# A recurrent layer's first run, moved beside the projection of its inputs and accumulated in PSUM

## The chip, the cores and the metric

The kernel runs on one core of one Trainium2 chip. The metric is the device time of one execution in microseconds (us); lower is better. The engines are named as in the profile: PE (TensorE, the matrix unit; PEld is its weight load), DVE (VectorE), ACT (ScalarE), POOL (GpSimd) and SP (SyncE, which only starts transfers here).

## The reference

A layer of two parts works on x with B = 2 sequences, T = 2048 steps and D = 256 features. First comes a normalized recurrent network, then attention with 8 heads of width 64 whose values and outputs are mixed from 5 experts each. Only the recurrent part is touched by the change:

```python
def _L0_attn_ref(x, Wi, bi, Wh, bh):
    xi = jnp.einsum('btd,hd->bth', x, Wi) + bi
    def step(h, xt):
        h_new = jnp.tanh(xt + h @ Wh.T + bh)
        return (h_new, h_new)
    h0 = jnp.zeros((x.shape[0], Wh.shape[0]), dtype=x.dtype)
    _, hs = jax.lax.scan(step, h0, jnp.swapaxes(xi, 0, 1))
    return jnp.swapaxes(hs, 0, 1)
...
x = x + _L0_attn_ref(_layernorm(x, axis=-1), ...)
x = x + _L0_ffn_ref(_layernorm(x, axis=-1), ...)
```

The entries of Wh are drawn with a spread of 0.02, so a state's influence fades quickly with the steps that follow it.

## The kernel before

All data are fp32. The kernel does not walk through 2048 steps one after the other. It cuts each sequence into 128 segments (NS) of 16 consecutive steps (S), and does step s of all 128 segments at once: one "chunk" c holds the 16-step position c of all segments of both sequences, 128 x 2 columns. The recurrent part then has these stages, in this order:

1. *Projection of inputs* (lines 277 to 335). For each of the 16 chunks: DVE measures mean and variance (`measure`), POOL normalizes, PE transposes (four 128x128 transposes, line 300), ACT copies the transposed chunk out of PSUM (line 302), PE multiplies it with Wi (two halves mc of the features, two halves kc of the contraction, line 309, 256 columns each), and ACT writes the sum plus both biases to `xi` in SBUF (line 316). The loop issues the transposes of chunk c+1 ahead of the projection of chunk c. `ps_xi` has three PSUM buffers for the products and `ps_t` three for the transposes.
2. *Run a, from zero states* (`run("a", ...)`, line 534, and `step`, line 358). It starts all segments from zero at position `SKIP` = 3, where the state is just tanh of `xi` (line 362), and does the positions 4 to 15 with one step each. A step does, for each batch b and each feature half mc, two matmuls with Wh over 128 columns (line 368), an addition of `xi` on DVE (line 375) and a tanh on ACT (line 376). Only the last states are kept, in `ends`, one column further to the right, so that the end of a segment becomes the start of the next.
3. *Run b* (`run("b", ...)`, line 535). It begins with the states in `ends` and does all 16 positions in the same way, keeping every state in `hs`. Beside it (`beside`, line 470) the states are transposed back, added to x on POOL, stored to DRAM, and normalized for the attention.
4. `compare` (line 505) subtracts the last states of run a from those of run b. If any of the 65,536 differs by more than `TOL` = 4 x 2^-23, a flag is set, and the whole pass is done again with `slow` set, where the segments are run 128 times over.

The attention follows, from about 110 us to the end; it is one long software-pipelined loop whose order is written out by hand.

Every stage touched here is under a manual schedule: each engine takes its instructions in the order in which the program writes them, and waits at each for what it needs. A matmul that waits holds back everything behind it on PE.

Of the kernel before, what the change touches and what calls it, by code (L numbers as in the profile page):

```python
# [8 lines left out]
F32 = mybir.dt.float32  # L9
I32 = mybir.dt.int32  # L10
AF = mybir.ActivationFunctionType
# [3 lines left out]
P = 128  # L15
EPS = 1e-5
PSUM = bass.MemoryType.PSUM
# [3 lines left out]
def pass_over(  # L21
# [17 lines left out]
    nc = tc.nc  # L39
    tc_pool, mark = tc.tile_pool, "s" if slow else ""  # L40

    def tile_pool(name, **kw):
        return tc_pool(name=name + mark, **kw)

    B, T, D = x.shape
    E, _, DH = Wv.shape
    H = Wq.shape[1] // DH
    KC = D // P
    NCH = T // P
# [32 lines left out]
    wh = rconst.tile([P, KC, D], F32, name="wh")  # L82
    bias = rconst.tile([P, 2, KC], F32, name="bias")
    bsum = rconst.tile([P, KC], F32, name="bsum")
# [42 lines left out]
    def misc(shape, nm):  # L127
        return ps_m.tile(shape, F32, tag="m", name=nm)
# [54 lines left out]
    def stats(pool, mv, src, nm):  # L183

        st = pool.tile([P, 6], F32, tag="ln_st", name=f"st{nm}")
        nc.vector.bn_stats(st, src)
        nc.vector.bn_aggr(mv, st)
# [26 lines left out]
    def scales(pool, mv, n, nm):  # L214

        neg, v, y = guess(pool, mv, n, nm)
        return neg, newton(pool, v, y, n, range(3), nm)

    def normalize(dst, src, neg, y, k, eng=nc.gpsimd):
        eng.tensor_scalar(  # L220
            dst, src, neg[:, k : k + 1], y[:, k : k + 1], ALU.add, ALU.mult
        )
# [39 lines left out]

    S = NCH
    NS = P
    NEWTON = 3


    rst = rw.enter_context(tile_pool(name="rst", bufs=1))
    xi = rst.tile([P, KC, S, B, NS], F32, name="xi")
    hs = rst.tile([P, KC, S, B, NS], F32, name="hs")  # L270

    ends = rst.tile([P, KC, B, NS + 1], F32, name="ends")
    ones = rst.tile([P, 1], F32, name="ones")
# [2 lines left out]

    with tile_pool(name="prep", bufs=3) as pp, tile_pool(
        name="lna", bufs=3
    ) as lnp, tile_pool(name="ps_xi", bufs=3, space=PSUM) as ps_xi, tile_pool(
        name="ps_t", bufs=3, space=PSUM  # L280
    ) as ps_t, tc.manual_schedule():
        norm_of, turned = {}, {}

        def measure(c0, n):
            mv = pp.tile([P, n * B, 2], F32, tag=f"mv{n}", name=f"mva{c0}")
            for c in range(c0, c0 + n):
                for b in range(B):
                    stats(lnp, mv[:, (c - c0) * B + b, :], xt[c][:, b, :], f"a{c}_{b}")
            neg, y = scales(lnp, mv, n * B, f"a{c0}")
            for c in range(c0, c0 + n):  # L290
                norm_of[c] = neg, y, (c - c0) * B

        def turn_in(c):
            neg, y, k = norm_of.pop(c)
            xn = pp.tile([P, B, D], F32, tag="xn", bufs=2, name=f"xn{c}")
            tp = ps_t.tile([P, KC, B, P], F32, tag="tp", name=f"tpa{c}")
            for b in range(B):
                normalize(xn[:, b, :], xt[c][:, b, :], neg, y, k + b)
                for kc in range(KC):
                    nc.tensor.transpose(tp[:, kc, b, :], xn[:, b, kc * P : (kc + 1) * P], ident)  # L300
            turned[c] = pp.tile([P, KC, B, P], F32, tag="xnT", bufs=2, name=f"xnT{c}")
            nc.scalar.copy(turned[c], tp)

        def project_in(c):
            xnT = turned.pop(c)
            for mc in range(KC):
                px = ps_xi.tile([P, B, P], F32, tag="px", name=f"px{c}_{mc}")
                for kc in range(KC):
                    nc.tensor.matmul(  # L309
                        px.rearrange("p b n -> p (b n)"),  # L310
                        lhsT=wi[:, kc, mc * P : (mc + 1) * P],
                        rhs=xnT[:, kc].rearrange("p b n -> p (b n)"),
                        start=kc == 0,
                        stop=kc == KC - 1,
                    )
                nc.scalar.activation(xi[:, mc, c], px, AF.Identity, bias=bsum[:, mc : mc + 1])

        groups, c0 = [], 0
        for n in (1, 1, 2, 3, 4, 5):
            groups.append((c0, n))  # L320
            c0 += n
        assert c0 == NCH
        measure(*groups.pop(0))
        nc.vector.tensor_tensor(bsum, bias[:, 0, :], bias[:, 1, :], ALU.add)
        for c in range(NCH):
            while groups and groups[0][0] <= c + 2:
                measure(*groups.pop(0))
            if c == 0:
                turn_in(0)
            if c < 2:  # L330
                project_in(c)
            if c + 1 < NCH:
                turn_in(c + 1)
            if c >= 2:
                project_in(c)

# [8 lines left out]

    TOL = 4 * 2.0**-23
    GC = NCH // 2
    SKIP = 3  # L350
    sp = rw.enter_context(tile_pool(name="step", bufs=3))
    lnp = rw.enter_context(tile_pool(name="ln", bufs=2))
    ps_t = ctx.enter_context(ExitStack())
# [3 lines left out]

    def step(nm, s, prev, h, ps_h):
        for b in range(B):
            if prev is None:  # L360
                for mc in range(KC):
                    nc.scalar.activation(h[:, mc, b, :], xi[:, mc, s, b, :], AF.Tanh)
                continue
            pre = sp.tile([P, KC, NS], F32, tag=f"pre{b}", name=f"pre{nm}_{s}_{b}")
            for mc in range(KC):
                ph = ps_h.tile([P, NS], F32, tag=f"ph{b}_{mc}", name=f"ph{nm}_{s}_{b}_{mc}")
                for kc in range(KC):
                    nc.tensor.matmul(  # L368
                        ph,
                        lhsT=wh[:, kc, mc * P : (mc + 1) * P],  # L370
                        rhs=prev(kc, b),
                        start=kc == 0,
                        stop=kc == KC - 1,
                    )
                nc.vector.tensor_tensor(pre[:, mc, :], ph, xi[:, mc, s, b, :], ALU.add)
                nc.scalar.activation(h[:, mc, b, :], pre[:, mc, :], AF.Tanh)  # L376

    def run(nm, from_zero, keep_states, ps_h, beside=None):
        prev = None if from_zero else (lambda kc, b: ends[:, kc, b, 0:NS])
        for s in range(SKIP if from_zero else 0, S):  # L380
            if keep_states:
                h = hs[:, :, s]
            elif s == S - 1:
                h = ends[:, :, :, 1:]
            else:
                h = sp.tile([P, KC, B, NS], F32, tag="h", name=f"h{nm}_{s}")
            step(nm, s, prev, h, ps_h)
            if beside:
                beside(s)
            prev = lambda kc, b, h=h: h[:, kc, b, :]  # L390

    def turn_back(c, nm):

        tp = pst.tile([P, B, KC, P], F32, tag="tp", name=f"tpb{nm}{c}")
        for b in range(B):
            for kc in range(KC):
                nc.tensor.transpose(tp[:, b, kc, :], hs[:, kc, c, b, :], ident)
        hv_of[c] = sp.tile([P, B, D], F32, tag="hv", bufs=2, name=f"hv{nm}{c}")
        nc.scalar.copy(hv_of[c], tp.rearrange("p b c d -> p b (c d)"))

    def add_back(c, eng):

        eng.tensor_tensor(xt[c], xt[c], hv_of.pop(c), ALU.add)  # L403
        nc.sync.dma_start(out=x1d[c], in_=xt[c])
# [4 lines left out]
    def roots(mv, n, nm, pool=lnp, split=False):  # L409
# [14 lines left out]
        yield  # L424
        for k in range(NEWTON):
            if y is None:
# [92 lines left out]
    with tile_pool(name="ps_h", bufs=1, space=PSUM) as ps_h:  # L519
        if slow:  # L520
            nc.gpsimd.memset(hs[:, :, S - 1], 0.0)
            with tc.For_i(0, NS, 1):
                nc.vector.tensor_copy(ends[:, :, :, 1:], hs[:, :, S - 1])
                run("c", False, True, ps_h)
            for c in range(S):
                turn_back(c, "c")
                add_back(c, nc.gpsimd)
                stats_back(c, "c")
            *_, root_of[0] = roots(mv2[0], GC, "c")
            for c in range(0, GC, 2):  # L530
                xn_of[c] = norm_back(c, "c", pool2)
        else:
            with tc.manual_schedule():
                run("a", True, False, ps_h)
                run("b", False, True, ps_h, beside)
                turn_back(S - 1, "b")
                for c in (S - 2, S - 1):
                    add_back(c, nc.vector)
                    stats_back(c, "b")
# [478 lines left out]
    for u, (i, n) in enumerate(units):  # L1018
        b, h = heads[i]
# [241 lines left out]
```

## Time and profile before

| | |
|---|---|
| Median of three runs | 1560.38 us (1559.92 to 1560.54) |
| Profiled execution | 1562.38 us |
| Its span, first to last instruction | 1560.5 us |
| PE busy | 1513.2 us (97%) |
| DVE busy | 1300.0 us (83%) |
| POOL busy | 1287.0 us (82%) |
| ACT busy | 1245.4 us (80%) |
| Projection of inputs | 0 to about 52.2 us |
| Run a | 52.9 to 74.4 us |
| Run b and what is beside it | 74.5 to about 110 us |
| Attention | to 1560.5 us |

The page of the profile lists engines, waits and the costliest groups of instructions. A name such as `px<-xnT,wi` is the tile that is written and those that are read; L309 is line 309 of the kernel. Nearly all of the span is attention, so shares over the span say little about the stages before it; those are read from the view by stretches of time and from the timelines of single engines. An fp32 matmul of the program shows as two records.

### The profile page before, as it was taken

How to read it: one execution, taken by the hardware profiler on the slowest of the kernel's cores; microseconds unless marked ns; L12 is line 12 of the kernel's file. 1: busy time of each engine (PE TensorE's matmuls, PEld its weight loads, DVE VectorE, ACT ScalarE, POOL GpSimd, SP SyncE). 2: the span in 40 equal slices, each digit the busy share in tenths (PEclk: the TensorE clock that was granted, in tenths of full speed). 3: DMA queues.
4: the chain of work that ended last, by engine and by line, in shares of the span. 5: the costliest groups of instructions: out<-in, count | busy, mean ns of one | idle time of the engine just before them, and what ended most of it. 6: DMA issues, size and time to landing. Idle time of an engine off the chain costs nothing.

```text
span 1560.5 us, 41474 instructions
## 1 busy us (share of the span) xinstructions
PE 1513.2 (97%) x17582; PEld 534.4 (34%) x17582; DVE 1300.0 (83%) x1811; ACT 1245.4 (80%) x1617; POOL 1287.0 (82%) x855
## 2 busy tenths in 40 slices
PE   6999899999999999999999999999999999999988
PEld 5984222222233333333223332222222222222233
DVE  7474899999988877888987779999999999899873
ACT  4674688888888888888887778888888888888863
POOL 3154699999999987999997778899999999999970
PEclk9999999999999999999999999999999999999999
DMA  5021478888888887788786777888888888888963
GB/s 167 1 109 40 114 163 196 190 189 176 177 178 179 183 183 162 163 178 179 160 200 156 167 161 176 175 178 176 175 177 179 175 179 180 174 170 176 195 163 92
DMA packets 86821, 254.15 MB, mean 163 GB/s; under 512 B 11808, under 2 KB 31072, under 8 KB 86624
## 3 DMA queue, kind: packets, MB, share of 16 engines
q0 software_dynamic: 43488, 164.65, 57.9%
q1 hardware_dynamic: 41504, 86.13, 16.6%
q8 instruction: 140, 2.29, 0.6%
q10 hardware_dynamic: 1632, 0.61, 0.2%
q14 instruction: 57, 0.47, 0.1%
HBM read 59.46 MB, written 50.33 MB: 70 GB/s over the span
## 4 chain that ended last, share of the span: by engine, by line
PE 63%; DVE 19%; ACT 7%; issue 5%; DMA 3%; POOL 1%; ACTq 0%; SPq 0%; DVEq 0%; POOLq 0%
PE s L642 21%; PE o L723 17%; DVE m L664 11%; ACT p L654 5%; PE d L744 4%; DVE pro L789 3%; PE pq L166 3%; PE pk L147 3%; PE pz L885 2%; PE phb L368 2%; PE px L309 1%; PE pha L368 1%; DMA p<-p 1%; DMA z<-x1d 1%; ACT p L713 1%
## 5 line engine op out<-in xcount | busy, mean ns | idle before, releaser
L710 POOL TENSOR_TENSOR p<-p,top 128x1024 f32<-128x1024 f32 x378 | 1005.1, 2759 | 25.8 <-ACT top L703 25.5
L654 ACT COPY p<-s 128x1024 f32<-128x1024 f32 x512 | 511.5, 1012 | 139.6 <-issue 60.8
L713 ACT ACTIVATE p<-p 128x1024 f32<-128x1024 f32 x512 | 538.8, 1064 | 51.3 <-DVE p L710 42.7
L642 PE MATMUL s<-q,k 64*32 64x512 f32 x4096 | 501.6, 596 | 4.9 <-ACT p L654 2.5
L642 PE MATMUL s<-qs,k 64*32 64x512 f32 x4096 | 501.6, 596 | 3.5 <-ACT p L654 1.8
L723 PE MATMUL o<-p,v 128*32 128x512 f32 x4096 | 492.4, 598 | 5.1 <-DVE os L760 4.3
L664 DVE TENSOR_TENSOR m<-s,m 128x1024 f32<-128x1024 f32 x320 | 390.7, 1221 | 85.5 <-PE s L642 76.1
L735 POOL DMA_DIRECT2D p<-p x254 | 259.9, 1023 | 103.2 <-issue 43.7
L723 PEld LDWEIGHTS o<-p,v 128*32 128x32 f32 x4096 | 114.0, 109 | 301.5 <-issue 158.9
L642 PEld LDWEIGHTS s<-q,k 64*32 64x32 f32 x4096 | 100.5, 106 | 156.0 <-ACT p L654 60.3
L642 PEld LDWEIGHTS s<-qs,k 64*32 64x32 f32 x4096 | 100.4, 106 | 154.2 <-ACT p L654 58.1
L710 DVE TENSOR_TENSOR p<-p,pt 128x1024 f32<-128x1024 f32 x126 | 152.4, 1210 | 0.0
L744 PE MATMUL d<-p,ones 128*32 128x512 f32 x1032 | 136.3, 592 | 1.6 <-DMA p<-p 1.6
L664 DVE TENSOR_TENSOR m<-s,p 128x1024 f32<-128x1024 f32 x64 | 78.4, 1225 | 50.5 <-ACT p L654 49.6
L789 DVE TENSOR_TENSOR pro<-po,mr 128x1280 f32<-128x1280 f32 (+1 forms) x67 | 95.9, 1431 | 3.2 <-DVE mr L785 0.5
L626 DVE TENSOR_TENSOR xq<-xq,wp 128x1280 f32<-128x1280 f32 x60 | 89.2, 1487 | 2.1
L632 DVE TENSOR_REDUCE v<-xq 128x256 f32<-128x1280 f32 x60 | 88.5, 1475 | 0.0
L166 PE MATMUL pq<-xn2T,wq 128*32 128x512 f32 x512 | 62.2, 598 | 0.0
L147 PE MATMUL pk<-xn2T,wk 128*32 128x512 f32 x512 | 61.5, 598 | 0.0
L744 PEld LDWEIGHTS d<-p,ones 128*32 128x32 f32 x1032 | 34.0, 110 | 79.9 <-issue 76.0
L843 POOL DMA_DIRECT2D yd<-pro x48 | 60.1, 1252 | 0.0
L403 POOL TENSOR_TENSOR x<-x,hvb 128x512 f32<-128x512 f32 x14 | 17.8, 1275 | 45.8 <-ACT hs L376 34.2
(178 smaller groups left out, 1492.3 us busy)
## 6 DMA issues: line engine op xcount, KB each, us to landing
p<-p POOLq DMA_DIRECT2D x254, 512.0 KB, 5.4
xq<-xvd SPq DMA_DIRECT2D x60, 640.0 KB, 4.3
yd<-pro POOLq DMA_DIRECT2D x48, 640.0 KB, 6.5
qs<-q SPq DMA_DIRECT2D x64, 128.0 KB, 4.8
yd<-pro SPq DMA_DIRECT2D x8, 640.0 KB, 5.9
y<-yd SPq DMA_DIRECT2D x8, 640.0 KB, 8.2
x<-in_x SPq DMA_DIRECT2D x16, 256.0 KB, 5.8
x1d<-x SPq DMA_DIRECT2D x16, 256.0 KB, 2.0
```

The lines of the kernel that those rows point to most:

```text
L147: nc.tensor.matmul(pk[at_col : at_col + 32], lhsT=wk[:, kc, h * DH + g : h * DH + g + 32], rhs=xc[:, kc, c0 // 2 : (c0 + HC) // 2, o, :], ...
L166: nc.tensor.matmul(pq[at_col : at_col + 32, :], lhsT=wq[:, kc, h * DH + g : h * DH + g + 32], rhs=xn2T[:, kc, b, n * QB : (n + 1) * QB], s ...
L626: nc.vector.tensor_tensor(xq, xq, wp.unsqueeze(2).to_broadcast([P, 4, DH, E]), ALU.mult)
L642: nc.tensor.matmul(ss[g : g + 32, o, :], lhsT=k_of[i][half, c, g : g + 32], rhs=q_of[i, n][o][half, :], start=True, stop=True, tile_positi ...
L654: nc.scalar.copy(p, ss)
L664: nc.vector.tensor_tensor(m, ss, ring[t - 1] if c == 1 else m, ALU.max)
L710: eng.tensor_tensor(p, p, top.unsqueeze(1).to_broadcast([P, 2, QB]), ALU.subtract)
L713: nc.scalar.activation(ring[t], ring[t], AF.Exp)
L723: nc.tensor.matmul(o_of[u][at_col : at_col + 32, :], lhsT=v_of[i][:, 2 * c + o, g : g + 32], rhs=ring[t][:, o, :], start=c == 0, stop=c == ...
L735: nc.gpsimd.dma_start(out=ring[t], in_=ring.pop(t + 1), accum_op=ALU.add)
L744: nc.tensor.matmul(den_of[u][32 * g : 32 * (g + 1), :], lhsT=ones32, rhs=ring[(t, t1)[g // 2]][:, g % 2, :], start=first, stop=last, tile_ ...
L789: nc.vector.tensor_tensor(dst, po[:, s : s + n, 0:DH].unsqueeze(2).to_broadcast([P, n, E, DH]), mr[:, s : s + n].unsqueeze(3).to_broadcast ...
```

## The change

Run a no longer follows the projection. A new function `first_run` does one position of it inside the projection's loop, one chunk behind. It multiplies the previous state of all 256 columns (both batches) with Wh straight onto the PSUM tile that holds that chunk's projection, without the start flag, and ACT takes tanh of the sum, with the biases, from PSUM. ACT still writes `xi` from the same tile first, since run b needs it. So that a PSUM bank is not shared, each product tile takes a full bank; there are six of them, and the transposes use the two buffers of the shared pool `misc` instead of three of their own. `run` and `step` keep only what run b and the repeated pass need. The order on PE in the loop becomes: transposes of chunk c+1, projection of chunk c, recurrent matmuls of chunk c-1.

```diff
@@ -262,6 +262,7 @@
     S = NCH
     NS = P
+    SKIP = 3
     NEWTON = 3
@@ -276,10 +277,8 @@
     with tile_pool(name="prep", bufs=3) as pp, tile_pool(
         name="lna", bufs=3
-    ) as lnp, tile_pool(name="ps_xi", bufs=3, space=PSUM) as ps_xi, tile_pool(
-        name="ps_t", bufs=3, space=PSUM
-    ) as ps_t, tc.manual_schedule():
-        norm_of, turned = {}, {}
+    ) as lnp, tile_pool(name="ps_xi", bufs=6, space=PSUM) as ps_xi, tc.manual_schedule():
+        norm_of, turned, px_of, h_of = {}, {}, {}, {}
@@ -293,7 +292,7 @@
-            tp = ps_t.tile([P, KC, B, P], F32, tag="tp", name=f"tpa{c}")
+            tp = misc([P, KC, B, P], f"tpa{c}")
@@ -303,17 +302,42 @@
         def project_in(c):
             xnT = turned.pop(c)
+            px_of[c] = []
             for mc in range(KC):
-                px = ps_xi.tile([P, B, P], F32, tag="px", name=f"px{c}_{mc}")
+
+                px = ps_xi.tile([P, 512], F32, tag="px", name=f"px{c}_{mc}")[:, : B * P]
                 for kc in range(KC):
                     nc.tensor.matmul(
-                        px.rearrange("p b n -> p (b n)"),
+                        px,
                         lhsT=wi[:, kc, mc * P : (mc + 1) * P],
                         rhs=xnT[:, kc].rearrange("p b n -> p (b n)"),
                         start=kc == 0,
                         stop=kc == KC - 1,
                     )
+                px = px.rearrange("p (b n) -> p b n", b=B)
                 nc.scalar.activation(xi[:, mc, c], px, AF.Identity, bias=bsum[:, mc : mc + 1])
+                px_of[c].append(px)
+
+        def first_run(c):
+
+            pxs, prev = px_of.pop(c), h_of.pop(c - 1, None)
+            if slow or c < SKIP:
+                return
+            h = ends[:, :, :, 1:]
+            if c < S - 1:
+                h = pp.tile([P, KC, B, NS], F32, tag="h", bufs=2, name=f"ha_{c}")
+            for mc, px in enumerate(pxs):
+                for kc in range(KC if prev is not None else 0):
+                    nc.tensor.matmul(
+                        px,
+                        lhsT=wh[:, kc, mc * P : (mc + 1) * P],
+                        rhs=prev[:, kc],
+                        start=False,
+                        stop=kc == KC - 1,
+                        skip_group_check=True,
+                    )
+                nc.scalar.activation(h[:, mc], px, AF.Tanh, bias=bsum[:, mc : mc + 1])
+            h_of[c] = h
@@ -333,6 +357,9 @@
             if c >= 2:
                 project_in(c)
+            if c:
+                first_run(c - 1)
+        first_run(NCH - 1)
@@ -357,10 +383,6 @@
     def step(nm, s, prev, h, ps_h):
         for b in range(B):
-            if prev is None:
-                for mc in range(KC):
-                    nc.scalar.activation(h[:, mc, b, :], xi[:, mc, s, b, :], AF.Tanh)
-                continue
@@ -375,15 +397,10 @@
-    def run(nm, from_zero, keep_states, ps_h, beside=None):
-        prev = None if from_zero else (lambda kc, b: ends[:, kc, b, 0:NS])
-        for s in range(SKIP if from_zero else 0, S):
-            if keep_states:
-                h = hs[:, :, s]
-            elif s == S - 1:
-                h = ends[:, :, :, 1:]
-            else:
-                h = sp.tile([P, KC, B, NS], F32, tag="h", name=f"h{nm}_{s}")
+    def run(nm, ps_h, beside=None):
+        prev = lambda kc, b: ends[:, kc, b, 0:NS]
+        for s in range(S):
+            h = hs[:, :, s]
             step(nm, s, prev, h, ps_h)
@@ -521,7 +538,7 @@
-                run("c", False, True, ps_h)
+                run("c", ps_h)
@@ -531,8 +548,7 @@
             with tc.manual_schedule():
-                run("a", True, False, ps_h)
-                run("b", False, True, ps_h, beside)
+                run("b", ps_h, beside)
```

More of the change, by code (lines that the diff above doesn't have):

```diff
@@ L335, in pass_over @@
                 project_in(c)
+            if c:
+                first_run(c - 1)
+        first_run(NCH - 1)
     TOL = 4 * 2.0**-23
     GC = NCH // 2
-    SKIP = 3
     sp = rw.enter_context(tile_pool(name="step", bufs=3))
```

## The prediction

> **What bounds the kernel now.** I read the view by stretches first, because the change touches only the first 75 us. Stretches 1 and 2 are the projection of inputs (before and after PE stops starving), 3 the hand-over to the run from zero states ("run a"), 4 run a, 5 the second run, 6 attention. Columns: length, then busy time and instruction count for PE, PEld, DVE, ACT, POOL, then clock, DMA share, GB/s.
>
> ```profile
> 0.00:24.13 24.13, 11.37 (x42) 7.96 (x42) 17.09 (x93) 6.46 (x11) 6.67 (x19) 1.00 0.91 270
> 24.13:52.16 28.03, 27.94 (x150) 24.15 (x150) 11.87 (x58) 18.77 (x37) 11.87 (x22) 1.00 0.00 1
> 52.16:52.91 0.75, 0.00 (x0) 0.00 (x1) 0.00 (x0) 0.72 (x3) 0.00 (x0) 1.00 0.00 0
> 52.91:74.62 21.71, 21.71 (x194) 21.71 (x195) 13.71 (x47) 14.88 (x50) 0.00 (x0) 1.00 0.01 2
> 74.62:110.60 35.98, 35.67 (x319) 35.27 (x318) 27.56 (x109) 26.95 (x83) 19.19 (x17) 1.00 0.26 96
> ```
>
> The projection has PE busy 27.94 of 28.03 us, run a 21.71 of 21.71. Both stages are bound by the same engine, so putting one beside the other overlaps nothing on PE. PE is idle only in the first 24 us, where the chunks wait for normalization.
>
> The chain that ended last stays on PE through these stages; PE's and ACT's timelines (start, length, engine, line, instruction, how many) give the borders:
>
> ```profile
> 30.51 0.86 PE L300 MATMUL tpa<-ident,xn 128*128 128x128 f32 x4
> 31.20 1.89 PE L309 MATMUL px<-xnT,wi 128*128 128x256 f32 x8
> 32.93 0.60 PE L300 MATMUL tpa<-ident,xn 128*128 128x128 f32 x4
> 33.37 1.89 PE L309 MATMUL px<-xnT,wi 128*128 128x256 f32 x8
> 35.10 0.60 PE L300 MATMUL tpa<-ident,xn 128*128 128x128 f32 x4
> ...
> 51.77 0.38 PE L309 MATMUL px<-xnT,wi 128*128 128x256 f32 x1
> 52.19 0.47 ACT L316 ACTIVATE xi<-px,bsum 128x256 f32<-128x256 f32 x1 [0.39 <-PE px L309]
> 52.56 0.90 ACT L362 ACTIVATE ha<-xi 128x128 f32<-128x128 f32 x4
> 52.91 1.94 PE L368 MATMUL pha<-ha,wh 128*128 128x128 f32 x15 [0.76 <-ACT ha L362]
> ...
> 74.45 0.94 PE L368 MATMUL phb<-ends,wh 128*128 128x128 f32 x7
> ```
>
> Since listed matmul lengths include pipeline drain, I count from start to start. A chunk's projection takes 35.10 - 33.37 = 1.73 us for 8 records, 0.217 us each. Run a takes 74.45 - 52.91 = 21.54 us for 192 records, 0.112 each: 1.795 us a step. (Each program matmul shows as two records.) The x4 transposes of chunk 7 take 0.26 us more than the next ones (0.86 against 0.60): POOL is late with its second half.
>
> [...] 128 columns 0.112 us a record, 256 columns 0.217, not 0.224[...]. [...] the trace's same-shaped L316 takes 473, which I use for the new tanh. [...]
>
> **The change, part by part.**
>
> 1. *Matmuls.* Run a loses 12 steps x 16 records x 0.112 = 21.54 us. The new run has, for the same 12 steps (chunks 4 to 15), 2 x 2 matmuls of 256 columns, 8 records of px's shape: 12 x 1.733 = 20.80. All of it lies on PE's path. Gain 0.74. Bounds: if the new records cost twice 0.112 the gain is nil; nothing suggests more than 0.74, since px already streams with these operands. I take 0.74.
>
> 2. *Chunk 7's late normalization.* The first recurrent matmuls (chunk 4) now stand in PE's order just ahead of chunk 7's transposes, so these come 1.73 us later and POOL is no longer late: gain 0.26 (0 to 0.26). Later chunks only gain slack on POOL. The starving before 24 us stays: the first recurrent matmul stands behind chunk 5's projection at about 30.7, so no hole before that is filled.
>
> 3. *The old hand-over goes.* From the end of px's last slot (51.77 + 0.217 = 51.99) to run a at 52.91: 0.92 us, in which ACT made the last xi and then tanh of step 3. Gain 0.92.
>
> 4. *New hand-overs.* Inside the loop, step c needs the tanh of step c-1, but between them PE does the next transposes (0.435) and projection (1.733). The tanh needs 0.03 us from PE's end to ACT's start (52.16 to 52.19), 0.47 on ACT, 0.04 to PE: 0.54. Counting 0.165 for the drain (0.38 - 0.217), slack is 2.17 - 0.71 = 1.46 us, so I cost it at nothing. ACT's queue there holds one copy (0.585), two xi (0.473 each), two tanh (0.473): 2.48 us per 3.90 us turn. Without this cover it would be 0.27 to 0.71 us a step. The cover ends with chunk 15: its first matmul needs only the first tanh of step 14, the second needs the one just issued. That is 0.165 + 0.54 - 0.433 = 0.27 us of waiting (0 to 0.71). Then the second run's first matmul waits. In the compiled order one wait stands on it and none on the second, so it waits for both last tanh: 0.165 + 0.54 = 0.705 us (0.48 if split like the others). Run a had no such gap, because its two batches alternate. Loss 0.27 + 0.705 = 0.975. Behind that waiting matmul stands the whole second run on PE, hence DVE and ACT too; nothing else to do exists.
>
> 5. *DVE, ACT, buffers.* DVE loses 48 adds at 0.292 us (14.0), ACT 52 tanh at 0.31 (16.1 summed), and ACT gains 26 tanh at 0.473 (12.3). None was on the path, as PE was full: nothing. Transposes move from three own PSUM buffers to the shared pool's two; a buffer is asked for two turns after its copy began, so no wait. px gets six banks instead of three: a bank is asked for after three chunks, and its tanh ran one turn after its projection plus about 0.5 us, again no wait. No DMA is added or moved.
>
> 6. *Everything behind.* POOL's and SP's orders are unchanged, and the second run and attention keep their instructions, so 1486 us should only start earlier.
>
> Sum: -0.74 - 0.26 - 0.92 + 0.975 = -0.95 us. The second run starts at 73.5 instead of 74.45; the span goes from 1560.5 to about 1559.55. The profiled execution took 1562.38 in all, 1.9 outside the span; the unprofiled median is 1560.38, so I forecast 1559.4.
>
> **The rivals.** A difference under 0.2% (3.1 us) is about what a measurement can't tell from no change, so my forecast counts as the same.
>
> *A. As summed*, 1559.4, own range 1558.8 to 1560.1: 0.70.
>
> *B. No gain on the matmuls* (adding into banks costs what the short ones did), 1559.4 + 0.74 = 1560.1: 0.08.
>
> *C. The runs really overlap*, run a's 21.5 us vanishing under the projection: 1560.4 - 21.54 - 0.26 + 0.06 (steps 2 to 4) = about 1538.7. It needs idle PE time inside the projection; the view shows 0.09 us in 28.03. Against: almost everything. 0.04, as the records' ends are modelled and PE may hold more room than it shows.
>
> *D. PE waits for ACT in every turn*, slower. Place: the first recurrent matmul of each chunk. If its wait were met only when ACT has done the newer chunk's xi (which comes after this turn's projection), each of 11 turns would lose about 0.705 us: +7.8, so 1567. It decides from about (3.1 + 0.95) / 11 = 0.37 us a turn. Against: the compiled order puts separate waits on the two halves of the state, as run a had, and the 1.46 us of slack. 0.03.
>
> *E. The pass is done twice*, slower. After the second run the kernel compares its last states with run a's, and if one differs by more than 4 x 2^-23 it repeats the pass step by step. Run a's sums are now rounded in another order (bias and recurrence on the PSUM sum) than the second run's. Price: at least 128 x 16 steps x 1.79 = 3,670 us plus attention's 1,450, so near 6,700. Worked out in ordinary fp32 arithmetic the largest difference is 1.5 x 2^-23 with either order, an estimate. [...] 0.02.
>
> *F. Attention doesn't keep its length.* The stage has 33 us without PE (1449.90 - 1416.54); another alignment of its DMAs could move the end by a few us either way: around 1556 (0.09) or 1564.5 (0.04). Against: three runs of before lie within 0.6 us.
>
> **How the numbers follow.** Faster by over 0.2%: C and the lower half of F, 0.13. Within: A and B, 0.78. Slower: D, E, upper F, 0.09. A and B hold 0.78 within 1558.8 to 1560.4; to reach 8 in 10 with the bounds of steps 1 to 4 (gain 0 to 1.9) and the near part of F, I take 1557.4 to 1560.8.
>
> **What would show it.** Step 1: the new matmul line has 96 records at px's spacing of 0.217. Step 2: chunk 7's transposes span 0.60. Steps 3 and 4: no gap on PE from 24 us until the last chunk, then about 0.3 and 0.7 us, both released by ACT's tanh; the second run's first matmul at 73.5. Step 6: first matmul of the second run to end of span stays 1486 us. I am wrong if PE shows waits for ACT in each turn, if the repeated part runs, or if attention's length moves by more than 1 us.

## The result, and the profile after

| | before | after |
|---|---|---|
| Median of 22 runs each | 1561.18 us | 1558.20 us |
| Ratio, with its 95% interval | | 0.9978 (0.9971 to 0.9984) |
| Span of the profiled execution | 1560.5 us | 1556.4 us |
| Second run's first matmul | 74.45 us | 73.45 us |
| PE busy / DVE busy | 1513.2 / 1300.0 us | 1510.6 / 1286.1 us |

The changed kernel is about 3 us faster, where 1.0 had been forecast. The 1558.20 lies in the range of 1557.4 to 1560.8, but outside the 1558.8 to 1560.1 that the sum alone was given. The prediction also took a difference under 0.2% as one that can't be told from none; with 22 runs each the interval shows this one clearly.

The view by stretches of the changed kernel, with the same columns as before (stretch, length, busy time and count of PE, PEld, DVE, ACT, POOL, clock, DMA share, GB/s). The first is the starved start, the second the projection with the first run beside it, the third the two new hand-overs, the fourth the second run:

```profile
0.00:24.13 24.13, 11.45 (x43) 8.06 (x44) 17.18 (x94) 6.46 (x11) 6.77 (x19) 1.00 0.90 269
24.13:70.78 46.65, 46.65 (x239) 41.10 (x240) 11.88 (x57) 29.68 (x61) 11.78 (x22) 1.00 0.01 1
70.78:73.45 2.67, 1.98 (x8) 1.07 (x7) 0.00 (x0) 1.42 (x3) 0.00 (x0) 1.00 0.00 0
73.45:109.70 36.25, 35.93 (x319) 35.55 (x319) 27.25 (x108) 26.38 (x81) 19.20 (x17) 1.00 0.26 96
```

In the second stretch PE has no idle time at all in 46.65 us. PE's timeline of the changed kernel around chunk 7's transposes (32.12), and at the end of the loop:

```profile
30.39 1.89 PE L331 MATMUL px<-ha,wh 128*128 128x256 f32 x8
32.12 0.60 PE L299 MATMUL tpa<-ident,xn 128*128 128x128 f32 x4
32.55 1.89 PE L310 MATMUL px<-xnT,wi 128*128 128x256 f32 x8
34.28 1.89 PE L331 MATMUL px<-ha,wh 128*128 128x256 f32 x8
...
68.87 4.02 PE L331 MATMUL px<-ha,wh 128*128 128x256 f32 x16
73.45 2.05 PE L390 MATMUL phb<-ends,wh 128*128 128x128 f32 x16 [0.56 <-ACT ends L339]
```

A recurrent step takes 34.28 - 32.55 = 1.73 us, as a projection does, and the transposes of chunk 7 are back at 0.60. The last two steps together span 4.02 us, where 2 x 1.73 and the drain of the last matmul (0.165) would be 3.63, and the second run then waits for ACT.

These first 73 us give 1.0 us. The spans of the two profiles differ by 4.1. The rest is in the closing part of attention (from the last copy of scores, at 1499.04 and 1497.72 us, to the end): 61.46 us before, 58.66 after, 2.8 less. The stretch between differs by 0.3. PE's timeline in the closing part of the kernel before:

```profile
1511.52 1.03 PE L744 MATMUL d<-p,ones 128*32 128x512 f32 x4
1513.63 0.62 PE L744 MATMUL d<-p,ones 128*32 128x512 f32 x2 [1.08 <-DMA p<-p]
...
1518.02 3.27 PE L723 MATMUL o<-p,v 128*32 128x512 f32 x16 [2.03 <-DVE os L760]
1521.21 1.17 PE L859 MATMUL py<-ident,y 128*128 128x128 f32 x6
```

The same place in the changed kernel:

```profile
1510.21 1.70 PE L760 MATMUL d<-p,ones 128*32 128x512 f32 x6
...
1515.73 1.92 PE L739 MATMUL o<-p,v 128*32 128x512 f32 x16 [2.10 <-DVE os L776]
1517.59 0.87 PE L875 MATMUL py<-ident,y 128*128 128x128 f32 x6
```

In the kernel before the sums (`d`) wait 1.08 us for an addition in transit, a transfer that adds one tile of `p` onto another on its way, and then the same 16 products (`o`) take 3.27 us instead of 1.92. The view by stretches says why. After the hole of 2.03 us the granted clock is 0.50 for 3.42 us:

```profile
1515.00:1518.45 3.45, 1.42 (x18) 0.50 (x15) 1.67 (x3) 0.00 (x0) 1.00 (x2) 1.00 0.78 190
1518.45:1521.87 3.42, 3.42 (x19) 1.14 (x12) 3.27 (x4) 1.06 (x1) 0.86 (x1) 0.50 0.97 274
```

The change touches none of this code. So the experiments ask two things: is the early part what the prediction said, and is the rest of the gain real, and where?

### The profile page after: what moved, and what is told of

It reads as the page before. It is cut to its first block, busy times and chain, and to the rows that moved or that the text cites. A ratio compares the mean times of both kernels' runs of the same rounds, so it can differ in the third digit from the quotient of the medians.

```text
span 1556.4 us, 41201 instructions
## 1 busy us (share of the span) xinstructions
PE 1510.6 (97%) x17486; PEld 530.0 (34%) x17486; DVE 1286.1 (83%) x1763; ACT 1241.6 (80%) x1591; POOL 1286.9 (83%) x855
## 4 chain that ended last, share of the span: by engine, by line
PE 64%; DVE 19%; ACT 7%; issue 5%; DMA 3%; POOL 1%; ACTq 0%; DVEq 0%; SPq 0%; POOLq 0%
PE s L658 22%; PE o L739 17%; DVE m L680 11%; ACT p L670 5%; PE d L760 4%; DVE pro L805 4%; PE pk L147 3%; PE pq L166 3%; PE pz L901 3%; PE phb L390 2%; PE px L310 1%; DMA p<-p 1%; PE px L331 1%; ACT p L729 1%; PE pv L597 1%
## 5 line engine op out<-in xcount | busy, mean ns | idle before, releaser
L397 DVE TENSOR_TENSOR preb<-phb,xi 128x128 f32<-128x128 f32 x64 | 17.9, 290 | 43.9 <-PE phb L390 43.7
```

## The experiments

Theory S held that the start of the second run gives 1.0 us and the rest is where half-speed windows fall. Theory R held that the kernel before is always slower in its closing part. "Mean loss of clock" below is the mean over a kernel's runs of 1 minus the granted clock of each, which is listed to three digits; a half-speed window of 3.4 us makes 0.0011 of it (3.4 x 0.50 / 1558). "Closing part" runs from the start of the last copy of scores to the end of the span, in the one trace that each kernel left. (The first two expectations let it begin at about 1484 us, 15 us ahead of that copy.)

The measure of clock is a rough one. Every trace also has a half-speed stretch in its last microseconds, behind PE's last matmul, where it costs PE nothing (from 1559.41 us in the kernel before and from 1552.53 in the changed one, with PE's last matmul over at 1554.26 and 1550.35); inside the span it lasts from 0.7 to 4.0 us, and so takes 0.0002 to 0.0013 of the loss.

### Both kernels again

No edit. These are second sets of runs and a second trace of each.

> The kernel before, unchanged, for a second trace and to see how far two sets of runs of one kernel lie apart. Theory S (the start of the second run is 1.0 us earlier, and the rest of the gain in the two profiles, 3.1 us, is a matter of where windows of the tensor clock fall in the closing part): ratio 1.000 within 0.0007; the trace has the second run's first matmul at 74.45 us again, while the closing part (from the last copy of scores at about 1484 us to the end) may differ from the first trace by up to 3 us, with or without a half-speed window. Theory R (the closing part of this kernel is always slower than that of the changed kernel): the closing part repeats its length of about 76 us and has its half-speed window again.

> The changed kernel, unchanged. Theory S: second run's first matmul at 73.45 us again; the closing part's length varies from trace to trace as in the kernel before; ratio between 0.9975 and 0.9995. Theory R: ratio 0.998 or less, and the closing part is again near 73.6 us without a half-speed window before the last few us.

The kernel before: 1561.94 us, 1.0005 (0.9998 to 1.0012). The changed kernel: 1558.69 us, 0.9984 (0.9977 to 0.9990). The gain is there again, at 2.5 us between the means (1561.18 for the 57 runs of the kernel before beside it, and 1558.66), above the 1.0 that the start explains. The starts repeat, at 74.39 and 73.64 us. The closing parts do not: 59.17 us for the kernel before, without a half-speed window ahead of the last microseconds, and 59.85 us for the changed kernel. So the 2.8 us of the first pair of traces is not a fixed property, and R as stated falls. But S isn't enough either. The two sets of 21 runs lie 2.8 us apart in their means, and runs of equal clock differ as well: with no loss listed, with 0.001 and with 0.002, the changed kernel is 2.2 us faster each time (21 runs against 71 of the kernel before).

### Buffers alone

```diff
-    ) as lnp, tile_pool(name="ps_xi", bufs=3, space=PSUM) as ps_xi, tile_pool(
-        name="ps_t", bufs=3, space=PSUM
-    ) as ps_t, tc.manual_schedule():
+    ) as lnp, tile_pool(name="ps_xi", bufs=6, space=PSUM) as ps_xi, tc.manual_schedule():
...
-            tp = ps_t.tile([P, KC, B, P], F32, tag="tp", name=f"tpa{c}")
+            tp = misc([P, KC, B, P], f"tpa{c}")
...
-                px = ps_xi.tile([P, B, P], F32, tag="px", name=f"px{c}_{mc}")
+                px = ps_xi.tile([P, 512], F32, tag="px", name=f"px{c}_{mc}")[:, : B * P]
```

> The kernel before with only the buffers of the change: each product of the projection takes a full PSUM bank, six of them, and the transposes use the two shared buffers. Run a stays where it was. Theory S: nothing, second run's first matmul at 74.4 to 74.5 us, ratio 1.000 within 0.0007. A rival that puts the gain on the buffers: the second run starts 0.3 us or more earlier, or the ratio is below 0.999.

1561.07 us, 1.0002 (0.9993 to 1.0011); second run from 74.56 us. The buffers alone do nothing that can be seen in the old order, as step 5 had said.

### The early gain given back

Unread matmuls in the loop of the changed kernel, behind chunk 10, or behind chunks 8 to 11:

```diff
+            if c in DELAY:
+                pd = misc([P, B, P], f"pd{c}")
+                for mc in range(2):
+                    nc.tensor.matmul(
+                        pd.rearrange("p b n -> p (b n)"), lhsT=wi[:, mc, 0:P],
+                        rhs=xi[:, 0, 0].rearrange("p b n -> p (b n)"), start=True, stop=True)
```

> The changed kernel with two more matmuls of 256 columns in the projection's loop behind chunk 10, whose product nobody reads: this gives back 2 x 0.433 = 0.87 us of PE time and changes nothing else. Theory S: second run's first matmul at 74.3 us, ratio 0.9995 to 1.0003 (what is left of the early gain is 0.1 us). Theory R, in which something other than the earlier start makes the changed kernel faster: the ratio stays near 0.9985, 0.87 us above that of the changed kernel.

> The changed kernel with two unread matmuls of 256 columns behind each of chunks 8 to 11: 8 x 0.433 = 3.46 us of PE time in the projection's loop. If the time follows the start of the second run one to one: start at 76.9 us, time 3.5 us over the changed kernel's (ratio 1.0005 with the whole difference counted at 2.9 us, 1.0016 at 1.0). If only the position in time decides, some steps of it cost nothing.

The short delay: 1560.29 us, 0.9994 (0.9985 to 1.0002). The long one: 1561.67 us, 1.0006 (1.0000 to 1.0013). From the first transposes of chunk 4 to the second run the traces show 52.48 and 55.08 us, against 49.94 in the changed kernel: 2.54 and 5.14 us more, where 0.87 and 3.46 had been put in. Each trace is of the slowest run of its list. Both hold an early half-speed window, to which the remaining 1.67 and 1.68 us are put down, and another one in the closing part. Here is the early one of the short delay (stretches as above, then PE's timeline):

```profile
21.90:25.30 3.40, 1.59 (x9) 1.25 (x10) 3.09 (x15) 0.90 (x2) 2.30 (x5) 1.00 0.52 119
25.30:28.70 3.40, 3.40 (x12) 2.73 (x11) 3.01 (x16) 1.53 (x3) 0.93 (x2) 0.50 0.00 0
...
23.61 0.97 PE L300 MATMUL tpa<-ident,xn 128*128 128x128 f32 x4 [1.91 <-POOL xn L220]
24.42 2.75 PE L311 MATMUL px<-xnT,wi 128*128 128x256 f32 x8
```

The hole in front of chunk 4, which traces of both kernels have, leaves PE busy for 1.59 of 3.40 us, and the next 3.40 us run at a granted clock of 0.50. Half the clock over 3.40 us in which PE is busy throughout comes to 1.70 us lost, by an estimate from this view. The remaining 1.67 and 1.68 agree with it, so apart from these windows the two delays passed through one to one. With the long delay the second run starts 2.6 us later than in the kernel before (3.46 - 0.87), yet the means of the runs are only 1.2 us apart (1562.46 against 1561.25 for 55 runs of the kernel before beside it). So even delayed, the changed kernel keeps some 1.4 us, with a standard error of 0.4, that its start doesn't explain; its ratio is the one expected if 2.9 us had been there to give back. For the short delay the same sum gives 0.7 with an error of 0.6, too large to decide.

### PE kept busy in two holes

In both kernels, four unread matmuls in front of chunk 4's transposes, and twelve in the closing part's hole:

```diff
+            if c == 2:
+                pw = misc([P, B, P], "warm_a").rearrange("p b n -> p (b n)")
+                ...  # four matmuls of 256 columns into pw
...
         project()
+        warm_b = other("warm_b")
+        for k in range(12):
+            g = 32 * (k % 4)
+            nc.tensor.matmul(warm_b[g : g + 32, :], lhsT=ones32, rhs=wq[:, 0, 0:QB],
+                             start=True, stop=True, tile_position=(0, g))
         products(tu)
```

> The kernel before with matmuls that nobody reads in two holes of PE: four of 256 columns (1.73 us) in front of chunk 4's transposes (hole from 21.6 to 23.5 us) and twelve small ones (about 1.3 us) in the closing part's hole of about 2 us. They should keep the windows of the tensor clock from falling to half speed there. Theory S (half-speed windows make the spread, and fall into the two kernels unequally): no half-speed window before the last microseconds, the spread of the runs shrinks, ratio 0.9985 to 0.9995. Rival (the clock has no part in it): ratio 1.000, the spread unchanged.

> The changed kernel with the same unread matmuls in the same two holes. Theory S: what is left between this and the kernel before with them is the earlier start alone, 0.7 to 1.4 us (ratios 0.0005 to 0.0009 apart). Rival (something in the changed kernel other than its start and the clock makes it faster): the two stay 2.5 to 3.4 us apart, ratio 0.998 against 1.000.

1560.63 us, 0.9994 (0.9986 to 1.0002), and 1558.36 us, 0.9981 (0.9973 to 0.9989). Neither trace shows a listed half-speed window ahead of the last microseconds, and the standard deviation of the runs falls to 0.76 and 0.74 us, from 1.25 for the kernel before beside them and 1.1 to 1.2 for the changed one. So these windows make a good part of the spread. But the two kernels still differ by 2.3 us in their medians and 2.0 in their means (standard error 0.3), not by 0.7 to 1.4. That speaks against S's account of the rest by clock windows alone. It doesn't settle it: in this pair of traces the second runs start 1.3 us apart (74.70 and 73.41), because in the kernel before the second projection took 3.78 us instead of 2.0 and the added matmuls then came late. How often the runs do that isn't known.

The clock of all runs says the same. The kernel before has a mean loss of 0.0013 to 0.0014 (57, 55 and 49 runs; 0.0018 in the 21 of its second set), the changed kernel 0.0010 (22 and 21 runs). Over all runs of all kernels here, a thousandth of loss goes with 0.9 us (a straight line with one slope). The windows then account for about 0.4 of the 2.9 us between the means. As part of the loss lies behind PE's last matmul, this is an estimate; at a window's full price in PE-bound work (1.67 us for 0.0011) it would be 0.6. Whether windows really fall less often into the changed kernel the traces don't show.

### The hand-over removed in the old order

Run a stays behind the projection with its 128-column matmuls, but step 3's tanh is taken inside the loop, and run a has PSUM buffers of its own, so that it needn't wait for the last chunk:

```diff
+    h3 = rst.tile([P, KC, B, NS], F32, name="h3")
+    ps_t = ctx.enter_context(ExitStack())
+    ps_h = ps_t.enter_context(tile_pool(name="ps_h", bufs=1, space=PSUM))
...
+            if c == SKIP + 1 and not slow:
+                for mc in range(KC):
+                    nc.scalar.activation(h3[:, mc], xi[:, mc, SKIP], AF.Tanh)
...
-        for s in range(SKIP if from_zero else 0, S):
+        for s in range(SKIP + 1 if from_zero else 0, S):
```

> The kernel before with the hand-over to run a removed by another way: run a stays behind the projection with its 128-column matmuls, but the tanh of step 3 is taken inside the projection's loop behind chunk 4, and run a's PSUM buffers are its own (the projection's products keep two, the transposes the shared two). Run a's first matmul then follows the projection at once: second run's first matmul at 73.5 us, 0.9 us earlier, without accumulation on the projection. If an earlier start is all: about as fast as its start says, ratio 0.9994; if any earlier start brings the larger gain: ratio 0.998; if the accumulation itself brings the rest: 0.9994 too, with the changed kernel staying at 0.998.

1558.52 us, 0.9984 (0.9977 to 0.9991). PE's timeline shows run a right behind the projection, and the second run at 73.15 us:

```profile
50.63 1.24 PE L311 MATMUL px<-xnT,wi 128*128 128x256 f32 x5
51.71 1.05 PE L367 MATMUL pha<-h,wh 128*128 128x128 f32 x8
...
73.15 0.83 PE L367 MATMUL phb<-ends,wh 128*128 128x128 f32 x6
```

From chunk 4's transposes to the second run it takes 49.78 us, against 50.81 in the kernel before and 49.94 in the changed one. With one hole of 0.9 us less, nothing accumulated on the projection and no wide matmul in run a, this kernel is as fast as the changed one. It also has a second gain that was not looked for: from the second run's start to the first copy of scores 53.86 us instead of 54.54. These two, 1.03 and 0.68, make 1.7 of the 2.6 us between its mean and that of before; again about 0.9 us is left over, with a standard error of 0.3. By the slope above, 0.3 of it goes with the clock. A leftover thus doesn't need accumulating in PSUM; that both kernels have it from the same cause is not shown.

### The closing part relieved

The closing part's transfers are all under way together: the DMA share of the kernel before is 1.00 from 1502 to 1515 us. Two of its loads (512 KB each) moved 10 and 14 turns ahead, into the first batch's part of `xn2T`, which is free by then:

```diff
-        load_z(B - 1, NQ - 3)
-        load_z(B - 1, NQ - 2)
...
+    at(behind, NT - 14, load_z, B - 1, NQ - 3)
+    at(behind, NT - 10, load_z, B - 1, NQ - 2)
...
-        z = ap.tile([P, QS, D], F32, tag="p1", bufs=RING[1], name=f"zz{b}_{n}")
+        if n < NQ - 1:
+            z = xn2T[:, n - NQ + 3, 0, 0 : QS * D].rearrange("p (s d) -> p s d", s=QS)
```

> The kernel before with two loads of the closing part (half a megabyte each, rows 4 to 11 of the saved x) moved out of it: they go to a part of the transposed input that is free by then, 10 to 14 turns earlier, where they no longer share the transfer engines with the last additions in transit. Theory C (the closing part waits for transfers that come late together, and does so more in this kernel than in the changed one): the closing part is 1 to 2 us shorter, ratio 0.9988 to 0.9994, and PE waits no longer for an addition in transit before the sums. Rival (the transfers there cost nothing): ratio 1.000.

> The changed kernel with the same two loads moved. Theory C: it gains less than the kernel before does, so that the two come within 0.9 to 1.4 us of each other, of which 0.87 is the start of the second run. Rival (the rest of the gain has nothing to do with transfers of the closing part): the two stay 2.5 to 3 us apart.

1558.75 us, 0.9986 (0.9980 to 0.9993), and 1557.48 us, 0.9975 (0.9967 to 0.9983). PE's timeline of the kernel before with the loads moved:

```profile
1511.14 1.04 PE L744 MATMUL d<-p,ones 128*32 128x512 f32 x8
1512.00 1.50 PE L888 MATMUL pz<-wo,yT 128*32 128x256 f32 x24
1513.45 1.92 PE L723 MATMUL o<-p,v 128*32 128x512 f32 x16
1515.31 0.88 PE L859 MATMUL py<-ident,y 128*128 128x128 f32 x6
```

Both waits are gone: the sums no longer wait for an addition in transit, and the hole of 2 us in front of the products is closed. The closing part takes 56.4 and 56.3 us. In the trace of the kernel before the closing part is 2.8 to 5.1 us shorter than in its other two, more than the 1 to 2 expected. The kernel before gains 2.6 us in the mean, the changed one 0.4 or 1.4, by which of its two lists one takes, and what remains between them is 1.2 us with a standard error of 0.3, as theory C had expected, but with a reservation. The changed kernel's 14 runs lost more clock here (0.0016 against 0.0010), and its trace holds an early half-speed window:

```profile
21.22:24.63 3.41, 1.40 (x8) 0.74 (x8) 3.04 (x16) 0.77 (x2) 1.46 (x3) 1.00 0.73 169
24.63:28.04 3.41, 3.41 (x11) 2.59 (x10) 3.10 (x15) 1.06 (x2) 1.78 (x4) 0.50 0.00 0
```

From chunk 4's transposes to the second run that trace takes 51.63 us instead of 49.94. At equal clock, by the 0.9 us per thousandth above, the two kernels would stand about 1.8 us apart, so half of the leftover may lie elsewhere. The run supports the closing part as a place of the larger gain; it doesn't prove it the only one. Nor does it tell two causes apart: the moved loads are issued well ahead of the additions, but they also no longer take buffers of the ring `p1`.

### The second run's PSUM buffers, and the best version

The one thing of the old-order run that could shorten the passage to attention: the second run's buffers laid ahead of those of the transposes, and freed together with them.

```diff
+    ps_h = ps_t.enter_context(tile_pool(name="ps_h", bufs=1, space=PSUM))
     pst = ps_t.enter_context(tile_pool(name="ps_tb", bufs=2, space=PSUM))
...
-    with tile_pool(name="ps_h", bufs=1, space=PSUM) as ps_h:
```

> The changed kernel with the second run's PSUM buffers laid first and freed only together with those of the transposes. In the run with the old order and no hand-over the stretch from the start of the second run to the first copy of scores took 53.86 us instead of 54.54, and this is the one thing it had there that others had not. If the placing of the buffers does it: 53.9 to 54.0 us here instead of 54.65, and 0.6 to 0.7 us off the time, ratio 0.9977 to 0.998. If not: 54.65 again.

> The changed kernel with both: the two loads moved out of the closing part, and the second run's PSUM buffers laid first. If the two gains add: stretch from the second run to the first copy of scores 53.97 us, closing part 56 to 57 us, time 4.3 to 4.8 us under the kernel before, ratio 0.997. If the earlier scores only wait elsewhere: ratio 0.9975 as with the loads alone.

The passage is shorter in the trace as expected, 53.97 us, but the time is 1558.67 us, 0.9985 (0.9978 to 0.9991), where 0.9977 to 0.998 was expected: its mean lies 2.6 us below that of before (standard error 0.4), the changed kernel's 2.5 (0.3). A gain of 0.7 is not seen, though this error doesn't quite exclude it. Together with the moved loads the passage takes 53.96 us and the closing part 56.4, and the time is 1556.00 us, 0.9969 (0.9957 to 0.9981), the best here and over 5 us below the kernel before, though from 6 runs only. Whether the 0.7 us is lost without the moved loads was not settled.

## Why the prediction was right or wrong

*Steps 1 to 5, the early part: right.* The forecast start of the second run was 73.5 us and it was 73.45 (73.64 in the second trace). The start of chunk 4's transposes also moves by some tenths from trace to trace (23.2 to 23.8 us where no matmuls were added in front), so the cleaner measure counts from there: 50.81 us in the two traces of the kernel before and in that of its buffer variant, and 49.94 after in both, a gain of 0.87 for a forecast 0.95. That the first pair of starts gave 1.0 was in part luck. By terms: the 256-column records came at px's spacing, so the 0.74 of step 1 stands. Step 2's 0.26 is seen in full (0.86 to 0.60). Step 4's waits were right too. With slots of 0.217 us the last step's second record pair began at 71.33 instead of 71.04, a hole of 0.29 (forecast 0.27). The last record began at 72.51, so its slot ended at 72.73, and the second run began 0.72 us later, at 73.45 (forecast 0.705). Not forecast were 0.10 us between the records at 71.33 and 71.65, which are 0.32 apart instead of 0.217. These terms come to a gain of 0.81; where the other 0.06 of the 0.87 lies was not looked for. The slack of 1.46 us inside the loop held: no wait at all. That DVE's and ACT's savings were worth nothing early on fits this sum.

*Rivals.* B falls with the spacing of 0.217. C falls, as PE was busy for the sum of both works, 46.65 us of 46.65. D falls, as PE shows no wait for ACT inside the loop. E didn't happen: a second pass would, by the forecast's estimate, have taken the time to some 6,700 us, and it was 1558.20. F was the direction of the surprise, "another alignment of its DMAs could move the end", given 0.09 at around 1556.

*Step 6 failed.* It said that the 1486 us behind the second run's start keep their length. They were 1486.05 and 1482.93 us in the first pair of traces and 1483.65 and 1483.84 in the second. So a single trace of the same kernel can be off by 2.4 us in this stretch, and the step rested on one. Over many runs the kernel is 2.5 to 3.5 us faster in the mean where the start gives 0.9 to 1.0. Of the other 1.5 to 2.5 us, about 0.4 goes with the clock, by the estimate above. A part may lie in the closing part, where moving the two loads brought the kernels to 1.2 us (at equal clock 1.8) of each other. The rest stays open. It doesn't need the accumulation, since the old order without the hand-over has a leftover too, and the buffers alone, in the old order, show no gain.

One more place shows in the traces. From the second run's start to the last copy of scores the kernel before takes 1424.5 to 1424.7 us in its two traces, with the buffer variant and with the loads moved, and the changed kernel 1424.0 to 1424.3 in its two and with the loads moved: 0.4 us less. With the added matmuls in both it is 0.1, and the delayed kernels as a whole don't show it. But a piece of 0.22 us is always at the same spot. DVE's timeline in the kernel before, then in the changed one:

```profile
1344.83 0.18 DVE L785 TENSOR_TENSOR mr<-po,gates_all 128x20 f32<-128x20 f32 x1
1345.26 1.49 DVE L789 TENSOR_TENSOR pro<-po,mr 128x1280 f32<-128x1280 f32 x1 [0.25 <-DVE mr L785]
...
1343.71 0.18 DVE L801 TENSOR_TENSOR mr<-po,gates_all 128x20 f32<-128x20 f32 x1
1343.92 1.49 DVE L805 TENSOR_TENSOR pro<-po,mr 128x1280 f32<-128x1280 f32 x1
```

All five traces of the old order with its hand-over have this wait, and a copy of scores that follows comes 0.22 us later; none of the other nine has it. Why code that was not touched waits there is not known.

In the traces with the closing part unchanged, the sums' wait for an addition in transit was 1.08, 0.55 and 0.53 us for the kernel before and its buffer variant. It was absent at this place in both traces of the changed kernel, but 1.53 us with the short delay and 0.36 us in the old order without hand-over. The second trace of the changed kernel has a longer one at the next sums:

```profile
1522.95 1.05 PE L760 MATMUL d<-p,ones 128*32 128x512 f32 x4 [1.75 <-DMA p<-p]
```

So the changed kernel isn't free of such waits, and why they come out differently was not found.

*The range held; the size was a third of what was measured.* That it held is in part luck: the sum's own range missed, and the wider one held because it took in part of F, whose cause wasn't forecast. The argument from three early runs within 0.6 us was too trusting: 22 runs of the same kernel spread over 4.4 us, with a median 0.8 us higher.

## What to carry to other kernels

Moving run a beside a projection that kept the same engine full bought no overlap (PE is busy for 46.65 of 46.65 us): it bought wider matmuls, one hidden normalization and one hand-over, each readable to 0.1 us from starts of neighbouring instructions, with the new hand-overs counted against them. Don't take the length of an untouched stretch from one trace: compare it in two traces of one kernel first. And before working on a stage of 75 us, look at the closing part: moving two loads out of it gave as much as the whole change.

## What the runs showed of the hardware

Holes of PE were followed by a granted clock of 0.50 for 3.40 to 3.42 us, but not all of them. A window cost 1.67 to 1.69 us in the PE-bound early part (three traces: 2.54 - 0.87, 5.14 - 3.46, 51.63 - 49.94).

How long PE was busy in the 3.4 us with the hole does not tell the two cases apart in these traces. A window followed 1.42 us busy of 3.45 in the closing part of the kernel before, 1.59 of 3.40 at the early hole of the short delay, and 1.40 of 3.41 at that of the changed kernel with the loads moved. In its second trace the kernel before has the hole in its closing part again (1.93 us in front of the products), and no window follows (the products take 1.92 us):

```profile
1514.16:1517.57 3.41, 1.48 (x20) 0.54 (x14) 1.59 (x3) 0.00 (x0) 1.69 (x2) 1.00 0.78 233
```

None follows in the first trace of the changed kernel either, where the hole in front of the products is 2.10 us long and the clock stays at 1.00:

```profile
1513.70:1517.10 3.40, 1.37 (x16) 0.50 (x16) 2.60 (x4) 0.23 (x1) 1.00 (x2) 1.00 0.75 173
1517.10:1520.50 3.40, 3.21 (x46) 1.64 (x42) 2.61 (x4) 2.73 (x6) 0.86 (x1) 1.00 1.00 240
```

So the hole in the closing part of the kernel before was followed by a window in one execution and by none in the next. What decides it is not shown. (PE's ends are modelled, and where a stretch is laid to begin moves these shares.)

The early hole itself comes and goes. In the second trace of the changed kernel the second projection took 3.78 us instead of 2.0, and PE reached chunk 4's transposes without a wait:

```profile
16.60 3.78 PE L310 MATMUL px<-xnT,wi 128*128 128x256 f32 x8 [0.67 <-ACT xnT L301]
20.17 1.33 PE L299 MATMUL tpa<-ident,xn 128*128 128x128 f32 x8
21.80 1.99 PE L310 MATMUL px<-xnT,wi 128*128 128x256 f32 x8 [0.29 <-ACT xnT L301]
23.70 0.44 PE L299 MATMUL tpa<-ident,xn 128*128 128x128 f32 x2
```

With both holes filled by unread matmuls, the two traces list no window ahead of the last microseconds, and the standard deviation of the runs fell from 1.25 to 0.76 us in the kernel before.
